# Seven buffers in place of eight for the pieces of x in the output phase of a two-layer selective-scan kernel

## The chip, the cores and the metric

The kernel runs on one core of one Trainium2 chip. The metric is the device time of one launch in microseconds (us); less is better. Where a profile is read, times are counted from the start of the profiled execution. The engines are called as in the profile: PE is TensorE, DVE is VectorE, ACT is ScalarE, POOL is GpSimd, and SP is SyncE, which here only issues transfers.

## The reference

Input x holds 8 images of 64 x 64 positions and 96 channels, in float32. Two layers follow each other, and each adds its result to x: a group norm over triples of channels, a projection to two halves of 192 channels, a 3 x 3 convolution of each channel with silu on the first half, a selective scan in four directions (rows, columns, and both reversed), a layer norm, a gate by silu of the second half, and a projection back to 96 channels.

```python
def _ss2d(x, ...):
    xz = x @ in_proj_w.T
    xp, z = (xz[..., :Di], xz[..., Di:])
    xc = _silu(conv3x3_depthwise(xp) + conv_b)
    xs = _cross_scan(xc)                      # 4 directions
    dts, Bs, Cs = split(einsum(xs, x_proj_w))
    delta = softplus(einsum(dts, dt_projs_w) + bias)
    # h = exp(delta * A) * h + delta * B * u;  y = sum over 16 states of h * C
    y = _cross_merge(_selective_scan(...), H, W)
    y = _layernorm(y, norm_g, norm_b)
    return y * _silu(z) @ out_proj_w.T
x = x + _L0_conv_ref(_gn(x), ...)
x = x + _L1_conv_ref(_gn(x), ...)
```

The second layer has the same frame; its scan divides by a decay that soon underflows, so that only the first positions of each direction contribute beyond a plain term.

## The kernel before, in words

The kernel goes through the images in order. For each image b there is a **scan phase** (scan_rows) and then an **output phase** (between, which calls out_phase). Every engine's instructions are issued in the order in which the program names them: a loop over steps calls, in each step, a hand-written list of stages, each with a lag, and no scheduler changes that order. Each queue, SP's for transfers included, is served in order.

The scan phase of image b treats the first layer's four directions in units of 1024 positions, and within a unit two halves of the channels in three groups each. A group has 32 channels x 4 states on the 128 partitions, and four such **sets** cover the 16 states. For a set, ACT makes the decay (L869), DVE multiplies the drive by B (L903; every fourth set POOL does that, L893) and runs the recurrence (L916), POOL multiplies by C (L932), and PE sums over states (L968). ACT also copies the drive (L886) once a group. What they read is loaded by SP: dt_rep and dtu_rep once a group (L526), b_rep and c_rep of each set once a unit (L536). Beside the sets, the next units are prepared: low_rows loads the rows for the step sizes of a unit (L557, into x_dbl0), PE makes the argument (L610), ACT takes it (L622, L623). A convolution of a later image or layer runs beside all this, on a strip called edged (set to zero by POOL at L1127, loaded at L1020, normalized by ACT at L1028).

Ahead of the first recurrence of a scan, SP issues in this order: dt_rep and dtu_rep of the first group, b_rep and c_rep of sets 0, 1 and 2, dt_rep and dtu_rep of the second group, b_rep and c_rep of set 3, then L557 and the load of edged (L1020). ACT's order there is: the drive's copy, the decays of sets 0 and 1, L622 and L623 for the argument, the state kept after set 0, the decay of set 2.

The output phase after image b's scan has, for b of 1 to 6, two streams one after the other in one pipeline: eight pieces of 512 positions of image b's first layer, then eight pieces of image b - 1's second layer. They are counted here as pieces 0 to 15. After image 0 there is the first stream alone; after image 7 the function finish has its own arrangement, in which only the second stream's pieces are loaded with loaded(). For piece c, the stages are in step c + lag:

- load of the piece of x into a tile x_in (lag 5, SP, L1590),
- products for the gate, ps_z, which read x_in (lag 7, PE, L1475), and their silu into sz, which has three buffers (lag 7, ACT, L1521),
- normalization and affine part (lag 8 and 9), product with sz (lag 9, POOL, L1534), the last reader of sz,
- projection ps_out (lag 10, PE, L1494) and the addition to x_in (lag 10, DVE, L1633 for the first stream, L1579 for the second),
- store of x_in (lag 11): pieces 0 to 7 on SP's queue (L1635), pieces 8 to 15 on ACT's queue (L1580).

At the end of every four pieces DVE refines an inverse root (newton, L1454 to L1456). The second stream also needs a map y1, loaded and patched in the first steps.

Tiles come from pools, and a pool's tiles get addresses in SBUF when it is opened; pools are opened and closed like a stack, from the left side or from the right. Where a tile of a later pool takes bytes that a tile of a closed pool had, its first writer waits for the last readers and writers of the old tile. In an output phase with two streams the pools on the left are, in order, xs (the buffers of x_in), behind (y1) and final (sz at its end). In the scan phase the left side holds x_dbl0 for L557, edged, the convolution's tiles and the scan's work tiles; on the right are the loads, of which dt_rep is the lowest.

Of the kernel before, what the change touches and what calls it, by code (L numbers as in the profile page):

```python
# [8 lines left out]
F32 = mybir.dt.float32  # L9
# [6 lines left out]
NB, HH, WW, C = 8, 64, 64, 96  # L16
# [6 lines left out]
MM = 512  # L23
# [27 lines left out]
def two_ss2d_layers(ctx: ExitStack, tc: tile.TileContext, t: dict, out: bass.AP):  # L51
# [1534 lines left out]

    def loaded(src, xpool):
        def chunk(i, pool):
            x = xpool.tile([C, MM], F32, name="x_in", bufs=8)
            nc.sync.dma_start(x, src[:, i * MM : (i + 1) * MM])  # L1590
            return x

        return chunk
# [348 lines left out]
```

## Time and profile before

| what | value |
| --- | --- |
| median of 3 runs | 12369.42 us (12340.3 to 12373.62) |
| profiled execution, its own time | 12341.47 us |
| its span, first to last instruction | 12339.6 us |
| mean granted TensorE clock | 0.81 of full |
| PE busy (matmul) | 9488.0 us, 77% |
| DVE busy | 10889.7 us, 88% |
| ACT busy | 9677.8 us, 78% |
| POOL busy | 10439.8 us, 85% |
| moved by DMA | 1861.52 MB, 151 GB/s in the mean |

The shares are of the whole span, over stages with different limits. A timeline view of one engine has one line for one instruction or for a merged row of equal ones: start, duration, engine, source line, operation, tiles, and in brackets the idle time ahead of it with what ended it. For a transfer, the duration is the time in which the queue issued it; its data moves after that. Engines are idle before an instruction for a cause that is named by its engine, tile and line, and a wait for several things is put down to the one that came last.

### The profile page before, as it was taken

To read this page: it belongs to the slowest core of one execution; us is meant where nothing else is said; L and a number is where in the kernel's file an instruction comes from. 1 tells how busy PE (TensorE), PEld (TensorE's weight loads), DVE (VectorE), ACT (ScalarE), POOL (GpSimd) and SP (SyncE) were. 2 spreads that over 40 slices of the span, in tenths; PEclk is the share of its full clock that TensorE was granted. 3 is DMA by queue.
4 is the path that set the end of the run, shared out by engine and by line. 5 is a ranking of instruction groups with operands and counts; after the bars stand their busy time and mean duration, and the time that the engine had idled before them with its cause. 6 is when DMAs were issued, how large, how long until landed. Compare 5 with 4: busy or idle time off the path is not lost. (4 is left out here: it accounts for less than half of the span.)

```text
span 12339.6 us, 134054 instructions
## 1 busy us (share of the span) xinstructions
PE 9488.0 (77%) x44276; PEld 3013.1 (24%) x44276; DVE 10889.7 (88%) x6819; ACT 9677.8 (78%) x15172; POOL 10439.8 (85%) x4748
## 2 busy tenths in 40 slices
PE   5875578887887778887788777888778887887567
PEld 1221122222222222222222222222222222222122
DVE  6999889997999969999699997999879998799985
ACT  4888778887787867888778787887878887788875
POOL 3999889996899969999699996999869998799973
PEclk8877778888888878888788888887888887888778
DMA  3444444444444444444444444444544445444441
GB/s 96 166 148 155 134 159 159 154 159 144 158 162 161 163 133 166 152 157 163 137 163 161 161 152 150 152 158 160 159 137 165 160 155 163 132 161 159 157 144 58
DMA packets 670623, 1861.52 MB, mean 151 GB/s; under 512 B 186824, under 2 KB 201454, under 8 KB 669917
## 3 DMA queue, kind: packets, MB, share of 16 engines
q1 hardware_dynamic: 662749, 1840.28, 45.1%
q10 hardware_dynamic: 7168, 12.59, 0.3%
q8 instruction: 351, 5.75, 0.2%
q14 instruction: 355, 2.91, 0.1%
HBM read 1539.31 MB, written 313.28 MB: 150 GB/s over the span
## 5 line engine op out<-in xcount | busy, mean ns | idle before, releaser
L932 POOL TENSOR_TENSOR out<-set,c_rep 128x1024 f32<-128x1024 f32 x3120 | 7295.1, 2358 | 905.9 <-DVE set L916 315.7
L916 DVE TENSOR_TENSOR_SCAN set<-decay,state,set 128x1024 f32<-128x1024 f32 x2304 | 5365.7, 2345 | 390.4 <-ACT decay L869 176.2
L869 ACT ACTIVATE decay<-dt_rep,w_a 128x1024 f32<-128x1024 f32 x3072 | 3420.2, 1114 | 332.9 <-DVE set L916 327.3
L903 DVE TENSOR_TENSOR set<-drive,b_rep 128x1024 f32<-128x1024 f32 x2352 | 2817.1, 1198 | 47.6 <-DMA b_rep<-x_dblr 39.1
L1035 PE MATMUL ps_conv<-edged,taps 96*96 96x512 f32 (+1 forms) x4032 | 2435.7, 743 | 54.7 <-ACT z L623 26.3
L968 PE MATMUL acc<-out,w_gather 128*32 128x256 f32 x24576 | 2271.9, 479 | 9.7 <-POOL out L932 9.6
L916 DVE TENSOR_TENSOR_SCAN set<-decay,set 128x1024 f32<-128x1024 f32 x768 | 1744.4, 2286 | 226.6 <-ACT decay L869 148.0
L893 POOL TENSOR_TENSOR set<-dtu_rep,b_rep 128x1024 f32<-128x1024 f32 x768 | 1811.2, 2358 | 97.0 <-DMA b_rep<-x_dblr 58.4
L959 PE MATMUL acc<-map,w_eye 96*32 96x256 f32 x4608 | 565.5, 572 | 1513.4 <-ACT map L998 1277.0
L998 ACT COPY map<-acc 32x256 f32<-32x256 f32 x3072 | 1472.7, 479 | 45.9 <-PE acc L968 5.6
L968 PEld LDWEIGHTS acc<-out,w_gather 128*32 128x32 f32 x24576 | 782.5, 130 | 1925.3 <-issue 1279.6
L1035 PEld LDWEIGHTS ps_conv<-edged,taps 96*96 96x96 f32 (+1 forms) x4032 | 718.8, 197 | 1383.1 <-issue 1220.3
L927 ACT COPY state<-set 128x1 f32<-128x1 f32 x2304 | 426.0, 185 | 761.4 <-DVE set L916 754.5
L642 PE MATMUL ps_sp<-z,w_eye 96*96 96x512 f32 x960 | 657.2, 773 | 287.9 <-ACT ln L651 244.6
L663 POOL TENSOR_TENSOR dtu<-ln,map 96x1024 f32<-96x1024 f32 x256 | 670.4, 2619 | 243.4 <-DVE ln L659 133.8
L886 ACT COPY drive<-dtu_rep 128x1024 f32<-128x1024 f32 (+1 forms) x816 | 813.6, 997 | 36.3 <-DMA dtu_rep<-dtu_far 31.0
L610 PE MATMUL ps_dt<-x_dbl,w_dtw 7*96 7x512 f32 x1024 | 594.7, 662 | 302.9 <-ACT z L623 150.9
L959 PEld LDWEIGHTS acc<-map,w_eye 96*32 96x32 f32 x4608 | 100.7, 120 | 1978.5 <-ACT map L998 1673.4
L642 PE MATMUL ps_sp<-dtu,w_eye 96*96 96x512 f32 x960 | 553.4, 661 | 0.0
L642 PE MATMUL ps_sp<-ln,w_eye 96*96 96x512 f32 x960 | 535.5, 642 | 0.0
L622 ACT ACTIVATE dt<-ps_dt 96x512 f32<-96x512 f32 x512 | 303.3, 592 | 279.7 <-PE ps_dt L610 261.0
L642 PE MATMUL ps_sp<-dt,w_eye 96*96 96x512 f32 x960 | 507.1, 611 | 0.0
(202 smaller groups left out, 9328.6 us busy)
## 6 DMA issues: line engine op xcount, KB each, us to landing
dt_rep<-dt_far SPq DMA_DIRECT2D x768, 512.0 KB
dtu_rep<-dtu_far SPq DMA_DIRECT2D x768, 512.0 KB
b_rep<-x_dblr SPq DMA_DIRECT2D x256, 512.0 KB
c_rep<-x_dblr SPq DMA_DIRECT2D x256, 512.0 KB
b_rep<-x_dblc SPq DMA_DIRECT2D x256, 512.0 KB
c_rep<-x_dblc SPq DMA_DIRECT2D x256, 512.0 KB
dt_far<-ln SPq DMA_DIRECT2D x256, 384.0 KB
dtu_far<-dtu SPq DMA_DIRECT2D x256, 384.0 KB
```

Of the source, the lines that this page charges most:

```text
L642: nc.tensor.matmul(job["ps"][:C, :], w["eye"], job[term][:, halves[s]], start=i == 0, stop=i == 3,)
L663: nc.gpsimd.tensor_tensor(like(job["dtu"], col), like(job["dt"], col), positions(xc[:, h, :], col, t0, T), ALU.mult,)
L869: nc.scalar.activation(s["decay"], s["group"]["dt"], AF.Exp, scale=rate)
L886: nc.scalar.copy(s["group"]["drive"], s["group"]["dtu"])
L893: nc.gpsimd.tensor_tensor(s["buf"], s["group"]["dtu"], b, ALU.mult)
L903: nc.vector.tensor_tensor(s["buf"], s["group"]["drive"], b, ALU.mult)
L916: nc.vector.tensor_tensor_scan(ordered(s["buf"], unit), ordered(s["decay"], unit), ordered(s["buf"], unit), 0.0 if unit["nth"] == 0 else s ...
L932: nc.gpsimd.tensor_tensor(s["out"], s["buf"], s["unit"]["c", s["i"]], ALU.mult)
L959: nc.tensor.matmul(acc, lhs[:, GC * g : GC * (g + 1)], positions(old[:, h, :], unit["column"], unit["t0"] + at, n), start=True, stop=False ...
L968: nc.tensor.matmul(acc, w["gather"], s["out"][:, at : at + n], start=False, stop=s["i"] == NS - 1, skip_group_check=True,)
L998: nc.scalar.copy(yk, like(acc, unit["column"]))
L1035: nc.tensor.matmul(job["ps"][:C, :], taps[l][:k, h, tap, :], edged[:k, tap // 3 : tap // 3 + rows, tap % 3 : tap % 3 + WW], start=tap == 0 ...
```

## The change

One number changes: the pool xs, or in finish the pool behind, holds seven buffers of [96, 512] for the pieces of x instead of eight.

```diff
     def loaded(src, xpool):
         def chunk(i, pool):
-            x = xpool.tile([C, MM], F32, name="x_in", bufs=8)
+            x = xpool.tile([C, MM], F32, name="x_in", bufs=7)
             nc.sync.dma_start(x, src[:, i * MM : (i + 1) * MM])
             return x
```

A buffer takes 2048 bytes of every partition, so all that is opened after it on the left side of an output phase begins 2048 bytes lower. In an output phase with two streams, x_in had bytes 109056 to 125440 and has 109056 to 123392; the third buffer of sz had 172864 to 176960 and has 170816 to 174912. The scan's lowest load, dt_rep, begins at 176096 in both kernels. The scan's x_dbl0 takes 109056 to 113152 in both, where the first two buffers of x_in were: of sixteen pieces these held 8 and 9 last, and hold 14 and 15.

The load of piece c + 8 took the buffer of piece c; now the load of piece c + 7 does.

## The prediction

> **What bounds the kernel now.** I read the page's busy shares first, then its groups, the table of waits, and last the timelines of the engines around one hand-over from an output phase to the next scan. The busy shares and the largest scan group of the page:
>
> ```profile
> PE 9488.0 (77%) x44276; PEld 3013.1 (24%) x44276; DVE 10889.7 (88%) x6819; ACT 9677.8 (78%) x15172; POOL 10439.8 (85%) x4748
> L916 DVE TENSOR_TENSOR_SCAN set<-decay,state,set 128x1024 f32<-128x1024 f32 x2304 | 5365.7, 2345 | 390.4 <-ACT decay L869 176.2
> ```
>
> VectorE is busiest and its time goes to the recurrences; so an idle VectorE inside a scan is lost time. The table of waits (total us, times, longest) says who kept it idle, and who kept that one idle:
>
> ```profile
> DVE set L916 <- ACT decay L869: 324.2, 196, 11.0
> ...
> ACT dt L622 <- PE ps_dt L610: 261.0, 309, 16.5
> ```
>
> Waits of 11.0 and 16.5 are not the scan's own rhythm, in which neighbours lie 1 to 4 us apart. They stand at the hand-overs. The VectorE timeline at the one after image 1 (start, duration, idle before with its releaser):
>
> ```profile
> 3078.08 0.69 DVE L1579 TENSOR_TENSOR x_in<-ps_out,x_in 96x512 f32<-96x512 f32 x1 [2.11 <-PE ps_out L1494]
> 3083.61 1.23 DVE L903 TENSOR_TENSOR set<-drive,b_rep 128x1024 f32<-128x1024 f32 x1 [4.84 <-DMA b_rep<-x_dblr]
> 3084.94 2.29 DVE L916 TENSOR_TENSOR_SCAN set<-decay,set 128x1024 f32<-128x1024 f32 x1
> ...
> 3101.88 2.29 DVE L916 TENSOR_TENSOR_SCAN set<-decay,set 128x1024 f32<-128x1024 f32 x1 [9.62 <-ACT decay L869]
> 3105.13 2.29 DVE L916 TENSOR_TENSOR_SCAN set<-decay,set 128x1024 f32<-128x1024 f32 x1 [0.96 <-ACT decay L869]
> ```
>
> The last addition of the output phase starts at 3078.08, the fourth recurrence at 3105.13: 27.05 us, with 15.7 of them idle. ScalarE tells why:
>
> ```profile
> 3078.80 0.33 ACTq L1580 DMA_DIRECT2D out<-x_in  x1
> 3082.11 1.02 ACT L886 COPY drive<-dtu_rep 128x1024 f32<-128x1024 f32 x1 [5.17 <-DMA dtu_rep<-dtu_far]
> 3083.06 2.15 ACT L869 ACTIVATE decay<-dt_rep,w_a 128x1024 f32<-128x1024 f32 x2
> 3099.67 0.59 ACT L622 ACTIVATE dt<-ps_dt 96x512 f32<-96x512 f32 x1 [14.47 <-PE ps_dt L610]
> ```
>
> It waits for the first load, and then at L622 for TensorE, whose L610 needs the rows that L557 loads. The third decay stands behind L622 on ScalarE. Now SP's queue and POOL:
>
> ```profile
> 3075.76 0.56 SPq L526 DMA_DIRECT2D dt_rep<-dt_far  x1
> ...
> 3087.56 0.28 SPq L557 DMA_DIRECT2D x_dbl<-x_dblr  x1
> ```
>
> ```profile
> 3073.39 2.34 POOL L1534 TENSOR_TENSOR y<-y,sz 96x1024 f32<-96x1024 f32 x1 [0.90 <-ACT y L1509]
> 3085.48 0.65 POOL L1127 MEMSET edged<- 96x660 f32 x1 [9.74 <-DMA out<-x_in]
> ```
>
> The first load is issued at 3075.76, when the last product that reads sz ends (3073.39 + 2.34 = 3075.73). That is the head of twelve loads of 512 KB (dt, dtu, b0, c0, b1, c1, b2, c2, the next group's dt and dtu, b3, c3; the digit is the set within the group), and the small L557 is behind them: issued at 3087.56, used by L610 at 3097.65.
>
> **What the Trainium skill says.** "Perfetto Trace Analysis", Optimization Strategy: a gap that repeats on the saturated engine can mean that there isn't enough SBUF for the next tile. It agrees: after images 1 to 6 the distance from the last L1579 to the fourth L916 is 27.05, 28.56, 28.06, 28.64, 28.43 and 26.94 us, 167.7 in all. "DMA: Bandwidth & Descriptors", Anatomy of one DMA: a semaphore wait is served on the issuing sequencer, ahead of dispatch. It agrees: everything later on SP waited with dt_rep. The same page, Issuing engines are not separate DMA queues: stores from ScalarE and loads from SP share 16 engines. It agrees: the last store, issued at 3078.80 in the burst, held the SP load that waits for it until 3085.36 (6.5 us), while the store below took at most 4.0. "SBUF — State Buffer", Who interferes with whom: DMA doesn't slow compute engines. L903 takes 1.23 us in the burst and 1.20 outside.
>
> **The change part by part.** *Instructions:* none is added, removed or reordered on any engine or queue; only waits and addresses differ.
>
> *The overlap removed.* The third sz buffer ended at byte 176960, in the dt_rep that begins at 176096; now it ends at 174912. In the changed program the first dt_rep waits for the last L1456 (3053.36 + 0.69 here), a variance product before it, and SP's own order: the load of piece 15 ahead of it. This concerns the six hand-overs after images 1 to 6. After image 0 there is one stream and no such overlap: priced at 0. After image 7 no such scan follows: 0.
>
> *Waits added: pieces.* Piece c+7 now waits for the store of piece c, one step earlier than c+8 did. What a lone store costs:
>
> ```profile
> 3046.59 0.32 SPq L1635 DMA_DIRECT2D x<-x_in  x1
> 3047.00 4.01 SPq L1590 DMA_DIRECT2D x_in<-x  x2
> ```
>
> The second of the two loads waited for that store and went at about 3050.6 (3047.00 + 4.01 - 0.42): at most 4.0 us. Behind such a wait stand the next store and loads on SP, whose turn is a step later. Piece 15 is tightest: store 8 leaves ScalarE at 3054.12, so its load goes at 3058.1 instead of 3050.6 and lands some 3.5 later (the first piece of the program: issued 25.3, read 28.8), at 3061.6; its gate products start at 3066.05. Cover 4.4 us; piece 14 has about 7, piece 13 about 10. So nothing, as long as the covers hold; image 7's phase likewise.
>
> *The burst moved.* dt_rep leaves at 3058.5 instead of 3075.76. In the old burst it landed after 4.5 us (3080.28, where SP takes the load that waits for it) and the others 1.7 apart (to 3088.85, five later). The same here gives dtu 3064.7, b0 3066.4, c1 3071.5, b2 3073.2. All transfers share eight semaphores by turns, and each waits for the one before it on its own: b2 for store 9 (3059.27 + 6.5 at worst, in time), b3 for store 11 (3068.03 + 6.5), c3 for store 12 (3070.40 + 6.5), so they land near 3080 and 3082. Wanted: dtu at 3079.1, b2 at 3087, b3 at 3086. All are in time.
>
> *Wait added: L557.* Its place now belongs to pieces 14 and 15, not 8 and 9; it waits for the last store. Behind it on SP: the load of edged; waiting for it: L610, L622, the third decay. Store issued 3078.80; lands +3.9 = 3082.7. L557's own landing isn't shown uncrowded: from below, the price in "DMA: Bandwidth & Descriptors", Anatomy of one DMA (stated for GpSimd's path), of 2.0 us and 28 KB over 436 GB/s, an estimate of 2.1; from above, 4.5 like dt_rep. I take 3.0: 3085.7. L610's pair 2.0 (3097.65 to L622 at 3099.67): L622 at 3087.7. From there as before, 2.21 to the third recurrence and 3.25 to the fourth: 3093.2, that is 15.1 us after L1579. POOL's L1127 waits for the same store, in both kernels: from 3082.7 its three memsets (1.5), L932 and L893 (2.35 each) end at 3089, ahead of the fourth recurrence. A sixfold sum: 167.7 - 6 x 15.1 = **77 us saved**.
>
> *Both ends.* Best: L557 hidden. Drive follows the store at 3079.15, L903 at 3080.2, recurrences 1.3, 4.8, 8.3 and 10.5 later: 12.6, saving 92. Worst: store 6.5, L557 4.5: 19.2, saving 52.
>
> Engines other than SP stood still in the gap too, so all move forward together. The profiled execution took 12341.5 (span 12339.6, 1.9 around it): 12264. The runs shown are 12340, 12369 and 12374: the median is 28 above it, which would give 12292. As the next median can come from either, I name 12280.
>
> **The rivals.** *The bubble only shrinks by half* (speaks for it: L557 and POOL's L1127 still wait for a store that then shares the engines with the end of the burst; against: the burst is mostly over by then). 40 us saved: 12302 from the profile, 12329 from the median.
>
> *The wait changes its name:* SP is held as long by piece 15, whose load now waits on ScalarE's store. It would have to go at 3075 instead of 3058; store 8 is out at 3054. No change: 12341 to 12369.
>
> *Slower: ScalarE's stores get stuck behind the burst.* Store 12 now waits for dtu, 14 for c1, 15 for b2 (shared semaphores), and ScalarE's queue holds affine, gate, drive and decay behind them. Covers by the times above: 5.7, 5.1 and 5.6 us. At a quarter of the old burst's rate (6.8 us a load) b2 would land near 3104, store 15 would be 25 us late and the distance 40: 6 x 12.2 = 73 us lost, 12414 from the profile. It decides where store 15 is late by the 12.9 us that the main case gains at a hand-over: at 4.8 us a load, 2.8 times the old burst's. That burst, crowded with the last stores, speaks against it.
>
> **How the numbers follow.** Main case 0.81, half 0.08, name only 0.05, slower 0.05, rest 0.01. 0.3% is 37 us, about what a measurement of this kernel tells from no change. Faster by more: main and most of half, 0.86; within: 0.08; slower: 0.06. Range: 12341 - 92 to 12374 - 52, widened by a few us for half: 12245 to 12325.
>
> **What would show it.** Right: dt_rep on SP some 17 us ahead of the last L1534; L886 without a DMA wait; L557 issued 4 us after the last L1580; L622's wait down from 14 to 16 us to about 5; distance L1579 to fourth L916 near 15 in all six; DVE's busy time unchanged. Wrong: gate products L1475 waiting for x_in, L1580 waiting for loads, or the distance still above 21.

## The result and the profile after

The changed kernel takes 12263.83 us in the median of 4 runs (12259.86 to 12269.9), the kernel before 12356.04 in the median of 4 (12340.3 to 12373.62). The ratio is 0.9929, with a 95% interval of 0.9914 to 0.9943: 0.7% faster, 92 us between the medians. The profiled execution took 12260.91 us (before: 12341.47), 80.5 less, at a granted clock of 0.811 (0.81). Two executions of the series further down, 14390 and 20714 us long at granted clocks of 0.56 and 0.505, are in a slow state and left out of every ratio and fit.

The page of the changed kernel, its line of busy shares and its largest group of recurrences:

```profile
PE 9486.1 (77%) x44276; PEld 3013.9 (25%) x44276; DVE 10892.5 (89%) x6819; ACT 9677.5 (79%) x15172; POOL 10438.3 (85%) x4748
L916 DVE TENSOR_TENSOR_SCAN set<-decay,state,set 128x1024 f32<-128x1024 f32 x2304 | 5366.1, 2345 | 408.0 <-ACT decay L869 201.1
```

The work is the same, to 3 us on VectorE and to the instruction on every engine. Only idle time went. The table of waits (total us, times, longest):

```profile
DVE set L916 <- ACT decay L869: 289.3, 203, 10.8
...
ACT dt L622 <- PE ps_dt L610: 178.9, 304, 15.1
```

ScalarE's wait at L622 lost 67 us: this row shows 82 of 261.0, but three waits of 5 us, 15.0 in all, now stand in a row of their own under POOL's L932. The longest that is left, 15.1, belongs to image 0. The instructions of L526 on SP's queue show the cause. Both rows give durations of the waits alone (ns, least, median, longest); the first is of the kernel before, the second of the changed one:

```profile
L526 SPq EVENT_SEMAPHORE  x1503: 17/17/21407, 196.2 to 12233.8; - x188
```

```profile
L526 SPq EVENT_SEMAPHORE  x1490: 17/17/985, 194.9 to 12153.0; - x187
```

A copy that stood up to 21.4 us at the head of SP's queue stands there at most 1.0 us now. The hand-over after image 1 on VectorE, ScalarE, SP and POOL, in that order, as they were shown for the kernel before:

```profile
3075.82 0.69 DVE L1579 TENSOR_TENSOR x_in<-ps_out,x_in 96x512 f32<-96x512 f32 x1 [2.11 <-PE ps_out L1494]
3078.01 1.23 DVE L903 TENSOR_TENSOR set<-drive,b_rep 128x1024 f32<-128x1024 f32 x1 [1.50 <-DMA out<-x_in]
...
3088.68 2.29 DVE L916 TENSOR_TENSOR_SCAN set<-decay,set 128x1024 f32<-128x1024 f32 x1 [2.44 <-ACT decay L869]
3091.93 2.29 DVE L916 TENSOR_TENSOR_SCAN set<-decay,set 128x1024 f32<-128x1024 f32 x1 [0.96 <-ACT decay L869]
```

```profile
3076.54 0.32 ACTq L1580 DMA_DIRECT2D out<-x_in  x1
3076.90 1.02 ACT L886 COPY drive<-dtu_rep 128x1024 f32<-128x1024 f32 x1 [2.24 <-DVE x_in L1579]
...
3086.48 0.59 ACT L622 ACTIVATE dt<-ps_dt 96x512 f32<-96x512 f32 x1 [6.48 <-PE ps_dt L610]
```

```profile
3054.01 0.32 SPq L1590 DMA_DIRECT2D x_in<-x  x1
3054.43 0.56 SPq L526 DMA_DIRECT2D dt_rep<-dt_far  x1
...
3082.36 0.28 SPq L557 DMA_DIRECT2D x_dbl<-x_dblr  x1
```

```profile
3071.13 2.34 POOL L1534 TENSOR_TENSOR y<-y,sz 96x1024 f32<-96x1024 f32 x1 [0.90 <-ACT y L1509]
3082.42 0.65 POOL L1127 MEMSET edged<- 96x660 f32 x1 [8.95 <-DMA out<-x_in]
```

The first copy of dt leaves right behind the load of piece 15 (3054.01, then 3054.43), 19.0 us ahead of the end of the last product (3071.13 + 2.34), where it used to leave with that end. ScalarE's copy of the drive (L886) no longer waits for a load. What is left is L622's 6.48 us: L557 leaves 5.8 us after the last store.

From the last L1579 to the fourth L916 it now takes 16.1, 14.8, 15.1, 14.5, 14.6 and 12.8 us after images 1 to 6, 87.9 in all against 167.7. That is 79.8 us, beside 80.5 between the two profiled executions. So close an agreement is luck: image 0's output phase ended 11.5 us earlier, and the stretches between the hand-overs together were 10.8 us longer. The first is no effect of the change. Image 0's last addition came at 1553.5 and 1559.2 us in two profiled executions of the changed kernel, at 1565.0 in kernel 8 below, which has seven buffers too, and at 1550.8 in kernel 3, which has eight.

### The profile page after: what moved, and what is told of

It is laid out like the page before. It is cut to its first block, busy times and chain, and to the rows that moved or that the text cites. A ratio compares the mean times of both kernels' runs of the same rounds, so it can differ in the third digit from the quotient of the medians.

```text
span 12259.1 us, 134056 instructions
## 1 busy us (share of the span) xinstructions
PE 9486.1 (77%) x44276; PEld 3013.9 (25%) x44276; DVE 10892.5 (89%) x6819; ACT 9677.5 (79%) x15172; POOL 10438.3 (85%) x4748
## 5 line engine op out<-in xcount | busy, mean ns | idle before, releaser
L932 POOL TENSOR_TENSOR out<-set,c_rep 128x1024 f32<-128x1024 f32 x3120 | 7296.1, 2358 | 892.6 <-DVE set L916 301.5
L916 DVE TENSOR_TENSOR_SCAN set<-decay,state,set 128x1024 f32<-128x1024 f32 x2304 | 5366.1, 2345 | 408.0 <-ACT decay L869 201.1
L903 DVE TENSOR_TENSOR set<-drive,b_rep 128x1024 f32<-128x1024 f32 x2352 | 2819.6, 1199 | 24.5 <-ACT drive L886 13.0
L916 DVE TENSOR_TENSOR_SCAN set<-decay,set 128x1024 f32<-128x1024 f32 x768 | 1744.5, 2286 | 166.0 <-ACT decay L869 88.2
L893 POOL TENSOR_TENSOR set<-dtu_rep,b_rep 128x1024 f32<-128x1024 f32 x768 | 1811.2, 2358 | 50.2 <-DMA b_rep<-x_dblc 14.9
L886 ACT COPY drive<-dtu_rep 128x1024 f32<-128x1024 f32 (+1 forms) x816 | 813.6, 997 | 19.4 <-DVE x_in L1579 13.5
L610 PE MATMUL ps_dt<-x_dbl,w_dtw 7*96 7x512 f32 x1024 | 589.8, 657 | 220.4 <-ACT z L623 150.8
L651 ACT COPY ln<-ps_sp 96x512 f32<-96x512 f32 x480 | 278.9, 581 | 267.9 <-PE ps_sp L642 261.0
```

Of the source, the lines that this page charges most:

```text
L886: nc.scalar.copy(s["group"]["drive"], s["group"]["dtu"])
L893: nc.gpsimd.tensor_tensor(s["buf"], s["group"]["dtu"], b, ALU.mult)
L903: nc.vector.tensor_tensor(s["buf"], s["group"]["drive"], b, ALU.mult)
L916: nc.vector.tensor_tensor_scan(ordered(s["buf"], unit), ordered(s["decay"], unit), ordered(s["buf"], unit), 0.0 if unit["nth"] == 0 else s ...
L932: nc.gpsimd.tensor_tensor(s["out"], s["buf"], s["unit"]["c", s["i"]], ALU.mult)
```

## The experiments

"Way" is the time from an output phase's last addition (L1579) to the start of the fourth recurrence (L916); a sum of ways is over the hand-overs after images 1 to 6. Ratios are to the kernel before, with 95% intervals. Where the trace merges two recurrences into one row, the second is put at its middle.

| kernel | ratio to before | sum of ways, us |
| --- | --- | --- |
| before | 1 | 167.7 |
| changed | 0.9929 [0.9914, 0.9943] | 87.9 |
| 1: larger spare tile, written | 1.0019 [1.0004, 1.0033] | 172.5 |
| 2: smaller spare tile, written | 0.9950 [0.9937, 0.9963] | 91.5 |
| 3: before, L557 early | 0.9990 [0.9977, 1.0004] | 165.7 |
| 4: changed, again | 0.9922 [0.9899, 0.9945] | 88.6 |
| 5: pools swapped | 0.9947 [0.9930, 0.9965] | 103.3 |
| 6: L610, L622, L623 a step later | 0.9942 [0.9919, 0.9964] | 77.1 |
| 7: image 0's stores on ScalarE | 0.9908 [0.9889, 0.9927] | 88.5 |
| 8: larger spare tile, not written | 1.0002 [0.9992, 1.0011] | 175.7 |
| 9: 7 and earlier deltas | 0.9921 [0.9908, 0.9934] | 90.7 |
| 10: 9 and 6 | 0.9921 [0.9908, 0.9935] | 78.5 |

### 1, 2 and 8: is it the address?

The theory of the prediction is that the gain comes from bytes alone: the output phase's pools ended above 176096, where the first dt_rep begins, and end below it now. The rival is that seven buffers help in another way. These kernels keep seven buffers and put the end back, or almost back, with a tile that nothing reads. Each kernel has one of the three added lines; the number behind # is the kernel's.

```diff
             plan, put = planner()
-
+            nc.gpsimd.memset(xpool.tile([C, 304], F32, name="spare")[:, 0:1], 0.0)   # 1
+            nc.gpsimd.memset(xpool.tile([C, 288], F32, name="spare")[:, 0:1], 0.0)   # 2
+            xpool.tile([C, 304], F32, name="spare")                                  # 8
```

> Seven buffers as in the changed kernel, with a spare tile of 1216 bytes per partition after them in the same pool, so that the output pipeline's pool ends at byte 176128 again, 32 bytes into the tile of the dt copies that begins at 176096. Overlap theory (the whole gain comes from the pool of the pieces no longer reaching into the pool of the next scan's loads): the first dt copy waits again for the last product of the output pipeline, the way from the last addition (L1579) to the fourth scan (L916) is 27 to 29 us again after images 1 to 6, and the time is that of the kernel before, 12356 us or so, up to 15 less because ScalarE's stores may meet fewer loads. Rotation theory (seven buffers help by another order of pieces and semaphores, the address doesn't matter): 12264 us, way 13 to 16 us.

> The same spare tile, 64 bytes smaller (1152 bytes per partition), so that the pool ends at byte 176064, 32 bytes short of the dt copies' tile. Overlap theory: the time of the changed kernel, 12264 us within 0.1%, way 13 to 16 us; the spare tile and its one-element write cost nothing. Rotation theory: the same 12264 us, so that only the pair with the larger spare tile decides; if this one is slow too, it's the spare tile itself and neither theory.

> The changed kernel with the spare tile of 1216 bytes in the pool of the pieces, as in the first experiment, but nothing is written to it, so that GpSimd has no wait of its own on it. Overlap theory, with the spare tile's write as the reason for the 23 us by which the first two experiments lay above before and after: the first dt copy waits for the last product L1534 again, the way is 27 to 29 us after images 1 to 6, and the time is that of the kernel before within 0.2%, seven buffers or not. Rotation theory: 12264 us.

Measured: kernels 1 and 2 differ by 64 bytes in the size of a tile, and by 81 us in their medians (12373.63 and 12292.63); their sums of ways differ by 81.0. Kernel 8, with seven buffers and the old end, is the kernel before: 1.0002. SP's queue and POOL of kernel 8 after image 1:

```profile
3074.52 0.56 SPq L526 DMA_DIRECT2D dt_rep<-dt_far  x1
```

```profile
3068.90 2.35 POOL L1534 TENSOR_TENSOR y<-y,sz 96x1024 f32<-96x1024 f32 x1 [1.80 <-ACT y L1509]
3072.16 2.34 POOL L1534 TENSOR_TENSOR y<-y,sz 96x1024 f32<-96x1024 f32 x1 [0.91 <-ACT y L1509]
```

The copy leaves at the end of the last product again (3072.16 + 2.34 = 3074.50). What follows: the overlap explains the whole gain, and the number of buffers does nothing else that these runs can see. One thing in it was unexpected. Only 32 bytes overlap, and they lie in the third buffer of sz. The program gives the pieces the three buffers in the order first, third, second, so the third was last read by the product of piece 13, which was over before 3068.90. The copy waited for the product of piece 15, which reads the first. So the wait is for the end of the old pool as a whole, not for the tile whose bytes are taken.

Kernels 1 and 2 were slower than expected: 1 by 0.17%, some 21 us, against 8, and 2 by 0.21%, some 26 us, against the changed kernel; in both pairs the intervals overlap a little. The one-element write, which I had priced at nothing, explains it. It heads POOL's work in each output phase and waits there for a store of an earlier phase; the list of what its line waits for (us, times), in kernel 2:

```profile
  DMA ys_far<-y_short: 35.1, 6
```

POOL's first sums (L1525) stand behind it, 5.9 us in each of six phases. From the end of a scan's last recurrence to the last addition of its output phase, the six phases take 1114.9 us in kernel 1 and 1125.6 in kernel 2, and 1087.7 to 1106.0 in all the others, kernel 8 among them.

### 3: is it the burst ahead of L557?

```diff
-                plan.setdefault(-1, []).insert(0, lambda: low_rows(x_dbl, units[1], rows))
+                plan.setdefault(-4, []).insert(0, lambda: low_rows(x_dbl, units[1], rows))
```

> The kernel before (eight buffers), with the load of the low rows (L557) issued from the plan's step -4 rather than -1, so that it stands ahead of the copies of b and c of sets 1 to 3 on SyncE's queue and not behind them. Theory that the way after the last addition is the 12 us of the burst of copies ahead of L557: with the burst still starting late, L557 is out some 4 us after the first dt copy and not 11.8 us, L610 and L622 come as much earlier, the way shrinks from 28 to about 21 to 24 us in six hand-overs, and the time is 12316 to 12331 us (25 to 40 us less than before). Rival, the copies of b and c themselves end last once the low rows are early (c of set 1 to 3 reach their scans late because they leave after L557): the way stays at 26 to 29 us, the time at 12350 us, and L916's waits name the DMA of b or c and not the decay.

Measured: 0.9990, and ways of 26.6 to 29.0 us. The gain of the first theory didn't come; of the rival, the ways came true, but VectorE's waits still name the decay. ScalarE and POOL after image 1:

```profile
3074.37 0.59 ACT L622 ACTIVATE dt<-ps_dt 96x512 f32<-96x512 f32 x1 [4.91 <-PE ps_dt L610]
...
3088.31 0.87 ACT L1028 ACTIVATE edged<-edged,gn_shift,gn_r 96x576 f32<-96x576 f32 x1 [11.77 <-DMA edged<-x]
```

```profile
3085.56 2.34 POOL L893 TENSOR_TENSOR set<-dtu_rep,b_rep 128x1024 f32<-128x1024 f32 x1 [10.86 <-DMA b_rep<-x_dblr]
```

L622 came 11.7 us after the last addition (3062.64), where it had been 21.6 in the kernel before. Then ScalarE stood for 11.8 us at L1028, whose strip is loaded by L1020, the load behind the burst that nobody had waited for as long as L557 was late too. The fourth set, which L893 makes on POOL, had stood almost as long for b3 and was ready at 3087.90, 0.4 us before ScalarE went on and 3.4 before the fourth recurrence (3091.34). So with L1020 early as well, at most some 3 us were to be had here: the burst itself ends late, as the rival says. With one small load moved, the wait went to the next one behind the burst; the change moved the burst. (After image 0, which the theories leave out, the way did fall, from 31.2 to 27.2 us.)

The same run corrects a step of the prediction. SP issued the first c_rep at 3062.22 and then stood until it issued L557:

```profile
3062.22 0.62 SPq L536 DMA_DIRECT2D c_rep<-x_dblr  x1
3070.33 0.28 SPq L557 DMA_DIRECT2D x_dbl<-x_dblr  x1
```

The last store was issued at 3063.35, and POOL's L1127, which waits for it too, started at 3070.39. So with eight buffers L557 waits for the last store as well. For this reason it left 10.0 us after the first dt copy (3060.31), not 4.

### 4 and 5: is what is left the wait of L557 for the last store?

Kernel 4 is the changed kernel again, on the chip of kernels 5 to 7.

> The changed kernel once more, beside the three kernels that follow, so that they can be set against it on one chip: every theory expects 0.9915 to 0.9945 of the kernel before.

```diff
-            tc.tile_pool(name="xs", bufs=1) as xpool,
             tc.tile_pool(name="behind", bufs=1) as pool,
+            tc.tile_pool(name="xs", bufs=1) as xpool,
```

> The changed kernel with its two pools opened in the other order, so that the tile of the low rows (x_dbl0, at byte 109056) lies in bytes that the second stream's map held, and no longer in bytes of the pieces of x. L557 then waits for the last product of the output pipeline and for its matmul L1494, not for the last store; the first L903 and the first L622 wait for the last store instead. Theory that what is left of the way (12.8 to 16.1 us) is set by L557 behind the last store: L557 is out 0.3 us or so before the last L1579 and not 4 to 6.5 us after it, the wait of L622 goes from 5 us to 2 or less, the way is 9.5 to 11.5 us after images 1 to 6, and the time 20 to 35 us below that of the changed kernel (12229 to 12244 us against 12264). Rival, the copies of b3 and c3 that wait for stores 11 and 12, or the edge load L1020, end last: L557 is early, but the way stays at 13 to 16 us with another name on the wait, and the time within 10 us of the changed kernel.

Measured: kernel 4 repeats the result (0.9922). In kernel 5 L557 leaves 0.03 us after the start of the last addition (3082.65 and 3082.62), as meant, but the ways grow to 15.0 to 18.6 us. VectorE of kernel 5 after image 1:

```profile
3082.62 0.69 DVE L1579 TENSOR_TENSOR x_in<-ps_out,x_in 96x512 f32<-96x512 f32 x1 [2.11 <-PE ps_out L1494]
3090.63 1.23 DVE L903 TENSOR_TENSOR set<-drive,b_rep 128x1024 f32<-128x1024 f32 x1 [7.32 <-DMA out<-x_in]
```

The last store, issued at 3083.34, now holds the first L903, whose tile took the bytes of the pieces, for 7.3 us. In the changed kernel the first two recurrences ran while L557 waited for its store. So in these kernels the last store limits the hand-over whether L557 or L903 waits for it, and the first instruction on the busiest engine is a worse place for that wait than a load. The ways are 2.5 us longer in the mean than kernel 4's; the two ratios point the same way, but their intervals overlap. Of the first theory only L557's early leave came true, and the rival named the wrong transfers.

### 6: the stalled engine does the recurrence's work first

```diff
-                            plan.setdefault(n + step, []).append(stage)
+                            plan.setdefault(n + step + (m == 0 and step < 3), []).append(stage)
```

> The changed kernel with the stages L610, L622 and L623 of the third job moved one step of the scan plan later, so that they stand behind the third decay on ScalarE. Theory that L622, waiting for the low rows with the third decay behind it, is what holds the third and fourth scan: the stall moves behind one scan more, the third scan no longer waits for it, the way to the fourth scan loses 1 to 3 us in six or seven hand-overs, and the time is 5 to 15 us below the changed kernel. Rival, ScalarE's work in these hand-overs is short of time as a whole (or the next stages meet the moved ones): no gain, within 5 us of the changed kernel, the third scan early but the fourth or fifth later by as much.

Measured: the third decay is ahead of the stall, and the ways are 12.8 to 13.0 us, 11.5 less in sum than kernel 4's. The time says nothing of it: 0.9942 and 0.9922 have overlapping intervals. How the saving fares further into the scan is seen by counting on. The mean over the six hand-overs of the time from the last addition to the start of a later recurrence, from the VectorE timelines:

| kernel | 4th | 8th | 16th | 32nd |
| --- | --- | --- | --- | --- |
| before | 27.9 | 40.7 | 66.7 | 120.5 |
| changed | 14.7 | 27.4 | 53.4 | 107.4 |
| 4, changed again | 14.8 | 27.5 | 53.5 | 108.2 |
| 5, pools swapped | 17.2 | 29.9 | 55.9 | 110.0 |
| 6, a step later | 12.8 | 26.2 | 52.5 | 107.2 |

The change's 13.3 us (79.8 over six) are still 13.1 at the 32nd recurrence. Of the 2 us of kernel 6, 1 is left at the 16th and, within what two runs of one kernel differ by, none at the 32nd. The rival's end came true, no gain, but not its place: the fourth and the eighth recurrence are still early. Which later wait takes the gain back was not tried.

### 7, 9 and 10: why image 0 gained nothing

```diff
-            return lambda: nc.sync.dma_start(x1[b][:, i * MM : (i + 1) * MM], x)
+            return lambda: (nc.sync if b else nc.scalar).dma_start(x1[b][:, i * MM : (i + 1) * MM], x)   # 7, 9, 10
...
-                steps += (8, 9, 9, 10, 10, 11, 12, 14, 15, 16, 16) + (11, 12, 12, 13)
+                steps += (8, 9, 9, 10, 10, 11, 12, *((14, 15, 16, 16) if b else (12, 13, 13, 13))) + (11, 12, 12, 13)   # 9, 10
```

The numbers behind # are those of the kernels that have the line; kernel 10 has kernel 6's line too.

> The changed kernel with the first image's stores of x1 (L1635, stream of image 0) put on ScalarE's queue as the stores of the other images' second stream are, where they were on SyncE's. Theory that the hand-over after image 0 gained nothing since its stores stand ahead of the loads on SyncE's queue: the first dt copy is then out some 17 us ahead of the last product, the way after image 0 falls from 31 to 14 to 18 us, and the time is 10 to 17 us below the changed kernel. Rival, it is the address and not the queue (the bytes of that hand-over lie elsewhere, and the dt copy waits for the last readers anyway): the way stays at 28 to 31 us and the time within 5 us.

Measured: the way after image 0 is 31.3 us, as in the kernel before (31.2) and the changed one (31.1). The ratio, 0.9908, can't be told from kernel 4's. SP's queue ahead of that scan:

```profile
1553.13 0.30 SPq L673 DMA_DIRECT2D dtu_far<-dtu  x1
1556.12 0.57 SPq L526 DMA_DIRECT2D dt_rep<-dt_far  x1
```

The queue of the stores isn't it. The copy reads what L673 has only just stored, and the next two kernels store that earlier. An output phase with one stream is half as long, and the next scan's deltas end with it.

> The changed kernel with the first image's stores of x1 on ScalarE's queue, and the second job's last stages (L630, the sums L657 to L659, the product L663, the stores L673) two or three steps earlier in the first image's output pipeline (steps 12, 13, 13, 13 for 14, 15, 16, 16). Theory that after image 0 the first dt copy waits for the deltas (L673 at 1553.13, the copy at 1556.12 in the run with the stores moved alone): the copy is out 6 to 10 us ahead of the last addition of image 0, L557 finds less of the burst ahead of it, and the way after image 0 falls from 31 us to 17 to 24 us; 7 to 14 us below the changed kernel. Rival, the burst is still ahead of L557 and L1020 whatever its start: the way stays within 3 us of 31.

> The same as the last one, and the stages L610, L622, L623 of the third job one step later in every scan as in the sixth experiment. If the two add up, the ways after images 0 to 6 lose 7 to 14 us and 14 us, and the time is 12236 to 12248 us against 12264 us for the changed kernel, a ratio of 0.990 to 0.992 to the kernel before. Rival, what they take out comes back in later waits of the scan: within 5 us of the changed kernel (0.9925 to 0.9935).

Measured: with earlier deltas the first dt copy of both kernels leaves 10.6 us ahead of image 0's last addition, where it had left 1.2 behind it, so no address holds it. The way after image 0 falls to 22.2 us in both, as expected, but the additions came later: the last at 1574.58 and 1567.21 (1559.22 in kernel 4), so that the fourth recurrence started at 1596.8 and 1589.4, against 1590.4. Most of this lateness was there before the output phase: image 0's scan ended at 1483.5 and 1476.2, against 1469.2 in kernel 4 and 1463.1 to 1477.3 in the others. The output phase itself took back 3.3 of the 9.0 us: from its first addition to its last it takes 39.2 us in both and 35.9 in every other kernel. At the 32nd recurrence kernel 9 is still 8.0 us nearer to the last addition than kernel 4 (115.0 and 123.0). A net gain of some 5 us, an estimate from these, is less than the ratios can show. Kernel 10 has short ways everywhere (78.5 and 22.2) and a ratio of 0.9921, the same as kernel 9's; it doesn't show that the two add up, and can't exclude it. No kernel here is shown to beat the changed one.

## Why the prediction was right, and where its reasons were not

**The sum.** A way was worked out at 15.1 us, 77 us saved; measured are 14.7 in the mean and 79.8 saved. Its terms, as predicted and as the trace of after has them:

| term | predicted | measured |
| --- | --- | --- |
| last store, issue to L557 | 3.9 | 5.8, 4.5, 4.6, 4.3, 4.2, 2.1 |
| L557 to L610 | 3.0 | 2.0 to 2.3 |
| L557 to L622 in all | 5.0 | 4.0 to 4.3 |
| L622 to the third and on to the fourth recurrence | 2.21 + 3.25 | 2.20 + 3.25 |

The uncrowded landing of L557 was mis-sized by about 1 us, since I took a middle between two bounds; the lower one, an estimate from the Trainium skill's "DMA: Bandwidth & Descriptors", Anatomy of one DMA, which states it for GpSimd's path, was 2.1, and the trace agrees with that (3082.36 to 3084.39). The store was mis-sized the other way, by 0.3 us in the mean, so the sum came out close. The shortest way, 12.8 after image 6, is the prediction's best case of 12.6: there the store took 2.1 us and the recurrences run without a gap.

**The time.** The sum gave 12264 from the profiled execution's own time, and that is what was measured (12263.8). To the microsecond this is luck: the profiled execution of the kernel before was 15 us faster than its new median (12341 and 12356), and the medians lie 92 us apart, 15 more than the 77. By the ratio's interval the gain is 70 to 106 us, which holds the 77 and the 79.8 of the ways alike. The 16 us that I added towards the median of 12369 were not needed: in the next runs the kernel before had 12356, and 12344 to 12354 in the experiments' series.

**Pieces waiting for stores** were rightly priced at nothing; the price of one was too high. Store 8 was issued at 3051.85 and piece 15's load went at 3054.01, 2.2 us later, not 4.0. The 4.0 was the dearest case to read: in four of the kernel before's six hand-overs the same wait is 2.0 us. So the copies left 21.4 us ahead of the last addition, where I had 19.6. The gate products (L1475) never wait for x_in in either trace.

**The burst** did what was written: b2, b3 and c3 each waited for the store named, which was issued 6.7, 7.7 and 6.5 us before (3057.00 to 3063.71, 3065.76 to 3073.48, 3068.14 to 3074.67). Two are longer than the 6.5 that I had called the worst; no recurrence waited for them.

**L557** is the step with a wrong reason. I called its wait for the last store an added one. It is not: kernel 3 shows it with eight buffers. It was there all along, over before L557's turn came behind the burst (SP's load of b3 had stood for the same store until 3085.36, and L557 left at 3087.56), and came out when the burst moved ahead. The time of the step was right, its reason was not. The description of the kernel is wrong at the same place. The program hands out a pool's buffers from the first on to the last and then downward, so that the first two, whose bytes x_dbl0 takes, held pieces 8 and 15 with eight buffers and hold 14 and 13 with seven. With seven, piece 15 lies at byte 121344, outside of x_dbl0, and L557 waits for its store all the same: a wait is for a whole pool, as in kernel 8, and not for the old tile alone.

**The rivals.** Half: refuted, the sum of ways would be 127.7 and is 87.9. A wait of another name: refuted, piece 15's load left at 3054.01, not near 3075, and the copies behind it stood at most 1.0 us. Slower through ScalarE's stores: the last store left 0.72 us after the start of the addition (3075.82 to 3076.54), as before (3078.08 to 3078.80). Of the marks of a right prediction, all held: the copy ahead by 19 us (17), L886 without a load, L557 4.2 to 5.8 us after the store (4) except for 2.1 after image 6, L622's wait 2.9 to 6.5 us (about 5).

## What to carry to other kernels

When the first loads of a stage all leave late, compare the addresses of their tiles with the end of the pools before: a few bytes of overlap cost a wait for a whole pool here, and 64 bytes were worth 81 us. A small load moved out from behind a burst gains only as much as the next thing that waits for the burst allows. After shortening a stall, count on to a much later instruction of the bounding engine, since a saving that is gone there is no saving.

## What was unexpected of the hardware

In these traces a transfer's landing depends on what was issued just ahead of it. L557 (28 KB) was used 10.1 to 11.9 us after its issue behind the burst of the kernel before, and 2.0 to 2.3 us after it in the changed kernel, where the burst's last copy had left 7.7 us earlier (image 1). In kernel 5, where that copy had left 1.1 us earlier, it took 5.9 us after image 1 (3082.65 to 3088.58) and 2.7 to 6.5 after the others. In kernel 3 the copies of sets 1 to 3 left right behind it, and it took only 1.9 to 2.4. All of these are after images 1 to 6. A store of a piece away from the burst was over in 2.0 to 2.2 us in ten of the twelve hand-overs of before and after, and in 4.0 and 4.1 in the other two; the three named above took 6.5 to 7.7 us among the 512 KB copies.

Executions of one kernel differ by up to 0.7%, and the longer ones tend to have the lower granted clock: kernel 4 took 12228 us at 0.815 and 12284 at 0.805. Fitted over 174 executions of the changed kernel, of the ten kernels and of the kernel before beside them, with a level of its own for each kernel, one lasts about 5 us longer for each 0.001 of the mean clock that it lacks (they lie between 0.799 and 0.817). The fit shows that the two go together, not which causes which. With this scatter, kernels that differ by 10 us in their ways can't be told apart by five executions of each.
